# Softmax weights of four key tiles summed on VectorE ahead of one product with ones, in five of sixteen attention steps

## The chip, the cores and the metric

One core of a Trainium2 chip runs the whole kernel in one launch. The time is the device time in microseconds (us) of that core, from launch to end. The kernel before takes 1580.93 us in the median of three runs (1577.99 to 1581.23). Nothing else runs beside it.

The engines of a core work from queues of their own, each in order: TensorE (PE in the profile, with the loads of its stationary operand shown apart as PEld), VectorE (DVE), ScalarE (ACT), GpSimd (POOL) and SyncE (SP), which only issues transfers here.

## What is computed

Two sequences of 1024 rows of 1024 numbers go through half a feed-forward block, an attention block and another half feed-forward block, each behind a layer norm and added to its input:

```python
x = x + 0.5 * ffn(layernorm(x), gate_w, base_w, base_b, lora_A, lora_B)
x = x + attn(layernorm(x), Wq, Wk, Wv, Wo)
x = x + 0.5 * ffn(layernorm(x), gate_w, base_w, base_b, lora_A, lora_B)
```

The feed-forward block is a 1024 x 1024 product with a bias and a low-rank part chosen by a gate. Attention has 32 heads of 32 numbers, 8 key and value heads (four query heads share one), rotary positions and a causal mask:

```python
att = einsum(q, k) / sqrt(32)                # causal, -inf above the diagonal
probs = softmax(att, axis=-1)
out = einsum(probs, v).reshape(B, T, 1024) @ Wo
```

The change lies in the divisor of that softmax: the sum of the exponentials over all keys of a row.

## The kernel before, in words

**Tiles and steps.** The 2 x 1024 rows are 16 tiles of 128 rows, numbered `t` from 0 to 15; tiles 0 to 7 are the first sequence, 8 to 15 the second. The program goes through 17 steps. A step does the attention of one tile, and beside it the dense work of other tiles: the feed-forward of tiles ahead (`stage_a1`), their projections to q, k and v (`stage_a2`), the output projection of the tile before (`stage_c1`) and the last feed-forward of an older tile (`stage_c2`). The strings `NORMAL` and `SEQS` set which pieces go into which step, and `step` hands them out between the units of attention. Tile 8 has its attention last, in step 16.

**A unit of attention** is a tile `t` and one key head `g` with its four query heads. Query tile `t` sees `L = t % 8 + 1` key tiles, so `L` is 4 for tiles 3 and 11, 5 for 4 and 12, and 8 for tile 7. Each unit passes twice over its key tiles:

- `unit_s1` (L634) makes the scores with queries on the partitions (PE, L649; four matmuls for a key tile) and takes their row maxima on VectorE (L666). The maxima are turned and go by four small transfers on SP (L685) into two extra rows of the query operand.
- `unit_s2` (L774) makes the scores the other way round, keys on the partitions, less the maxima (PE, L782), and their exponentials on ScalarE (L788) as a tile `p32` of 128 keys x (4 heads x 128 queries) in 32-bit floats. On the diagonal GpSimd zeroes what is masked (L790).

**Values and divisors.** `av_add` (L747) collects the `p32` tiles of a unit in batches of up to four (`BATCH`). When at least two more key tiles have followed (`SKEW`), `av_batch` (L709) issues the products of a batch as one unbroken run on PE (L727), each held behind the one before. A batch of four key tiles has four products with the values, `(0, VA[..], p32)`, and then products with a matrix of ones, `(1, ones, sums)`, which add up the exponentials over the 128 keys. For the latter, `add_pairs` (L694) first adds the exponentials two key tiles at a time on VectorE (L706) into a buffer `pair`, of which there are two. Such a product is four matmuls, one for a head, each with a stationary operand of 128 x 32 at a column position of its own; in the trace each matmul is two records, so one product is eight records. A key tile left over, without a partner, goes to its ones product as it is. After a unit's last batch, ScalarE copies both results (L734), VectorE takes the reciprocal (L736) and the product (L741), and L742 and L743 split it in halves for the output projection.

**What sets the order.** The order of the instructions on each engine is not that of the text alone. The program is laid out by a scheduler that goes by times it assumes for each instruction, held in places by explicit orders (the run of `av_batch`, and dense work kept behind the L782 matmuls by `behind`). So an instruction more on one engine can move others, also in steps that the edit doesn't name.

**Weights.** The projections' weights lie in device memory in halves of 1 MB and are fetched on SP by `prefetch` (L414, issue L418) into three buffers `ws` in turn. A fetch waits on SP until the products that read its buffer are through. SP carries all other loads too: the query rows (L685), the inputs `xt` (L136) and the stores of results (L819, L821).

Of the kernel before, what the change touches and what calls it, by code (L numbers as in the profile page):

```python
# [13 lines left out]
ALU = mybir.AluOpType  # L14
# [18 lines left out]
AHEAD = 5  # L33
NEARLY = 3
LOFF = 2
NTURN, NTURN2 = 3, 3
TLAG = 12
SB, LB = 3, 2
# [3 lines left out]
def kernel(  # L42
# [16 lines left out]
    nc = tc.nc  # L59
# [574 lines left out]
    def unit_s1(t, g):  # L634
# [8 lines left out]
        for j in reversed(range(L)):  # L643
            ps = p_s1.tile([P, GRP, P], FP, name="s1")
            diag = j == L - 1
            off = diag and L > LOFF
            pem = diag and not off
# [44 lines left out]
    pairs = {}  # L692

    def add_pairs(batch):  # L694

        t, g, L, us = batch
        key = (t, g, us[0][0])
        if key in pairs:
            return
        pairs[key] = []  # L700
        for i in range(0, len(us), 2):
            if i + 1 == len(us):
                pairs[key].append(us[i][1])
                continue
            sums = pp.tile([P, GRP, P], FP, name="pair", bufs=2)
            nc.vector.tensor_tensor(sums, us[i][1], us[i + 1][1], ALU.add)  # L706
            pairs[key].append(sums)

    def av_batch():  # L709

        add_pairs(pend[0])
        t, g, L, us = pend.popleft()
        if us[0][0] == 0:
# [33 lines left out]
    def av_add(t, g, j, L, p32):  # L747

        if not pend or len(pend[-1][3]) == BATCH or pend[-1][0:2] != (t, g):
            pend.append((t, g, L, []))  # L750
        pend[-1][3].append((j, p32))
        after = 0
        while len(pend) > 1:
            after = sum(len(b[3]) for b in list(pend)[1:])
            add_pairs(pend[0])
            if after < SKEW:
                break
            av_batch()
# [367 lines left out]
```

## Time and profile before

| what | value |
|---|---|
| median of three runs | 1580.93 us |
| the profiled execution, its own time | 1578.13 us |
| its span, from first to last instruction | 1576.3 us |
| mean granted TensorE clock | 0.983 |
| busy: PE, DVE, ACT, POOL | 1488.0, 1120.9, 893.6, 381.0 us |
| DMA, mean rate over the span | 136 GB/s |

The profile is taken of one execution. Busy time is a union: two records that overlap on an engine are counted once. The matmuls' ends are modelled and overlap the next ones, so the mean duration of one is longer than its share of the engine; the distance from start to start says what one costs. The chain that ended last is followed back from the last instruction: what it gives as a line's share is the time in which that line's instructions were what the end waited for. A row "A <- B" in the view of the waits says that engine A stood idle until instruction B ended.

The attention steps can be told in the trace by the exponentials at L788, of which tile `t` has 8 x `L`. Step 3 runs from 286.2 to 381.8 us, step 4 to 479.3, step 7 from 696.6 to 871.5, step 11 from 1019.2 to 1116.6 and step 12 to 1214.1.

### The profile page before, as it was taken

Reading aid. Unit: us, or ns where it says so; the run is one execution under the profiler, and the core shown is the slowest. Engines: PE = TensorE matmul, PEld = TensorE weight load, DVE = VectorE, ACT = ScalarE, POOL = GpSimd, SP = SyncE. Lnnn points to the kernel's source line nnn. Section 1 sums busy time; section 2 is a strip of 40 time slices with the busy share of each in tenths; the row PEclk is TensorE's granted clock in tenths of the full one; section 3 lists DMA queues with packets and bytes.
Section 4 is the critical chain, followed back from the end, with each engine's and each line's share of the span. In section 5 each row is a group of like instructions: output and inputs, shape, how many; then the busy total and the mean of one; then the engine's idle time right before and its main releaser. Section 6 shows DMA issues by size and latency. Waiting matters only on the chain.

```text
span 1576.3 us, 38332 instructions
## 1 busy us (share of the span) xinstructions
PE 1488.0 (94%) x15908; PEld 865.4 (55%) x15908; DVE 1120.9 (71%) x2454; ACT 893.6 (57%) x1523; POOL 381.0 (24%) x636
## 2 busy tenths in 40 slices
PE   5898999999999999989999898999999999999998
PEld 3345556555565555656554454655555556566644
DVE  6777668757587686787744575766869688689653
ACT  8575546556466465565642545554746556566731
POOL 3342333222132231221211122222222122221120
PEclk9998999999999999999999999999999999999999
DMA  8943163262522603513526324345170431601241
GB/s 292 327 134 135 55 227 109 70 249 57 216 95 91 232 14 122 189 42 138 188 76 251 121 95 161 122 156 167 44 277 17 181 129 31 248 27 69 82 161 41
DMA packets 57501, 214.25 MB, mean 136 GB/s; under 512 B 19952, under 2 KB 23024, under 8 KB 37872
## 3 DMA queue, kind: packets, MB, share of 16 engines
q1 hardware_dynamic: 51248, 184.54, 32.6%
q0 software_dynamic: 4640, 16.78, 5.8%
q10 hardware_dynamic: 1440, 10.49, 1.6%
q8 instruction: 125, 2.05, 0.5%
q14 instruction: 48, 0.39, 0.1%
HBM read 191.34 MB, written 20.19 MB: 134 GB/s over the span
## 4 chain that ended last, share of the span: by engine, by line
PE 74%; DVE 11%; ACT 7%; issue 2%; DMA 2%; POOL 1%; SPq 0%; DVEq 0%; ACTq 0%; POOLq 0%
PE pd L406 14%; PE pd L407 14%; PE pd L408 14%; PE av L727 11%; PE s L782 6%; PE s L649 6%; DVE mx L666 3%; PE s L332 3%; ACT p L788 2%; DVE bst L382 1%; DMA ws<-wstr 1%; DVE pair L706 1%; DVE o L736 1%; ACT tt L333 1%; DVE ws L208 1%
## 5 line engine op out<-in xcount | busy, mean ns | idle before, releaser
L788 ACT ACTIVATE p<-s,cs 128x512 f32<-128x512 f32 x576 | 378.0, 690 | 163.5 <-PE s L782 160.8
L666 DVE TENSOR_REDUCE mx<-s 128x4 f32<-128x512 f32 x480 | 313.9, 674 | 80.1 <-PE s L649 70.3
L706 DVE TENSOR_TENSOR pair<-p,p 128x512 f32<-128x512 f32 x256 | 178.9, 701 | 80.9 <-ACT p L788 31.4
L782 PE MATMUL s<-qt,kts 98*128 98x512 f16 x576 | 207.4, 387 | 16.8 <-ACT p L788 9.5
L649 PE MATMUL s<-kts,qt 96*128 96x128 f16 x2304 | 210.3, 223 | 11.2 <-DVE mx L666 8.3
L406 PE MATMUL pd<-ws,tt 128*128 128x512 f16 x544 | 206.4, 380 | 2.5 <-DMA ws<-wstr 1.0
L649 PEld LDWEIGHTS <-qt 96*128 96x128 f16 x2304 | 161.4, 99 | 85.4 <-issue 39.9
L407 PE MATMUL pd<-ws,tt 128*128 128x512 f16 x544 | 206.1, 379 | 0.0
L408 PE MATMUL pd<-ws,tt 128*128 128x512 f16 x544 | 205.3, 379 | 0.0
L406 PE MATMUL pd<-wb,tt 128*128 128x512 f16 x512 | 197.8, 386 | 6.3 <-DVE xt L493 4.9
L407 PE MATMUL pd<-wb,tt 128*128 128x512 f16 x512 | 197.1, 385 | 1.3 <-DVE wb L208 1.3
L408 PEld LDWEIGHTS <-tt 128*128 128x128 f16 x1312 | 128.7, 98 | 125.9 <-issue 7.8
L407 PEld LDWEIGHTS <-tt 128*128 128x128 f16 x1312 | 129.5, 99 | 122.3 <-issue 14.3
L408 PE MATMUL pd<-wb,tt 128*128 128x512 f16 x512 | 196.4, 384 | 0.0
L406 PEld LDWEIGHTS <-tt 128*128 128x128 f16 x1312 | 129.0, 99 | 122.1 <-issue 11.3
L727 PE MATMUL av<-p,va 128*32 128x128 f32 x4608 | 167.2, 278 | 5.1 <-POOL p L790 3.8
L727 PEld LDWEIGHTS av<-p,va 128*32 128x32 f32 x4608 | 115.2, 110 | 74.4 <-issue 50.7
L743 POOL TENSOR_TENSOR tt<-o,tt 128x128 f16<-128x128 f32 x128 | 61.3, 479 | 372.3 <-ACT tt L742 366.0
L790 POOL TENSOR_SCALAR_AFFINE_SELECT p<-p 128x512 f32<-128x512 f32 x128 | 82.6, 647 | 260.4 <-ACT p L788 256.4
L736 DVE RECIPROCAL o<-o 128x128 f32<-128x128 f32 x128 | 120.5, 942 | 22.9 <-ACT o L734 22.7
L661 POOL TENSOR_SCALAR_AFFINE_SELECT sm<-sm 128x512 f32<-128x512 f32 x96 | 71.1, 741 | 229.0 <-ACT sm L660 218.6
L333 ACT COPY tt<-s 128x1024 f16<-128x1024 f16 x84 | 84.3, 1019 | 34.3 <-PE s L332 33.8
(203 smaller groups left out, 2175.0 us busy)
## 6 DMA issues: line engine op xcount, KB each, us to landing
ws<-wstr SPq DMA_DIRECT2D x142, 1024.0 KB
xt<-hb POOLq DMA_DIRECT2D x32, 512.0 KB, 5.5
wstr<-ws ACTq DMA_DIRECT2D x9, 1024.0 KB
xt<-in_x_dram SPq DMA_DIRECT2D x16, 512.0 KB
out_dram<-xt SPq DMA_DIRECT2D x15, 512.0 KB
qt<-mt SPq DMA_DIRECT2D x256, 1.0 KB
ws<-in_wb_dram SPq DMA_DIRECT2D x2, 1024.0 KB
qst<-in_wb_dram SPq DMA_DIRECT2D x2, 1024.0 KB
```

The lines of the kernel that those rows point to most:

```text
L333: nc.scalar.copy(out, ps[0:rows])
L406: nc.tensor.matmul(ps, lhsT=th, rhs=wh, start=(k == 0), stop=False)
L407: nc.tensor.matmul(ps, lhsT=th, rhs=wl, start=False, stop=False)
L408: nc.tensor.matmul(ps, lhsT=tl, rhs=wh, start=False, stop=(last and k == KB - 1))
L649: nc.tensor.matmul(ps[:, h, :], lhsT=q[0 : 3 * DH, h, :], rhs=KT[b0 + j][0 : 3 * DH, g, :], start=(not pem or h == 0), stop=not pem,)
L666: nc.vector.tensor_reduce(mx[:, odd, j, :], ps, AX.X, ALU.max)
L706: nc.vector.tensor_tensor(sums, us[i][1], us[i + 1][1], ALU.add)
L727: prev = nc.tensor.matmul(av[rows, i, :], lhsT=w, rhs=p32[:, h, :], start=(us[0][0] == 0 and n == 0), stop=(last and n == len(runs) - 1), ...
L736: nc.vector.reciprocal(rc, rc)
L782: ins = nc.tensor.matmul(ps.rearrange("p h k -> p (h k)"), lhsT=KT[b0 + j][0 : MR + MC, g, :], rhs=q[0 : MR + MC].rearrange("p h k -> p (h ...
L788: nc.scalar.activation(p32, ps, AF.Exp, scale=cs)
L790: nc.gpsimd.affine_select(out=p32, in_=p32, compare_op=ALU.is_ge, fill=0.0, base=0, pattern=[[0, GRP], [1, P]], channel_multiplier=-1,)
```

## The change

In the steps of tiles 3, 4, 7, 11 and 12, when a batch has a second pair, its sum is added to the sum of the first pair, in place, and only the sum of all four key tiles is kept for a product with ones.

```diff
+QUAD = [3, 4, 7, 11, 12]
...
             sums = pp.tile([P, GRP, P], FP, name="pair", bufs=2)
             nc.vector.tensor_tensor(sums, us[i][1], us[i + 1][1], ALU.add)
+            if i == 2 and t in QUAD:
+                nc.vector.tensor_tensor(sums, sums, pairs[key].pop(), ALU.add)
             pairs[key].append(sums)
```

Line numbers in the text are those of the kernel before. In the changed kernel the lines below the new constant are one further down, the new addition is its L709, and what follows it is three further down (the matmuls of `av_batch` at L730).

## Prediction

> **What bounds the kernel now.** I read the busy shares first, then the chain that ended last, then the steps of the change, then the lines that it touches.
>
> ```profile
> PE 1488.0 (94%) x15908; PEld 865.4 (55%) x15908; DVE 1120.9 (71%) x2454; ACT 893.6 (57%) x1523; POOL 381.0 (24%) x636
> ...
> PE 74%; DVE 11%; ACT 7%; issue 2%; DMA 2%; POOL 1%; SPq 0%; DVEq 0%; ACTq 0%; POOLq 0%
> PE pd L406 14%; PE pd L407 14%; PE pd L408 14%; PE av L727 11%; PE s L782 6%; PE s L649 6%; DVE mx L666 3%; PE s L332 3%; ACT p L788 2%; DVE bst L382 1%; DMA ws<-wstr 1%; DVE pair L706 1%; DVE o L736 1%; ACT tt L333 1%; DVE ws L208 1%
> ```
>
> TensorE holds the end: it is busy for 94% and carries 74% of the chain. L727, the line that loses work, is on the chain for 11%; L706, which is like the line that gains work, for 1%. An average over stages doesn't say this of the five steps, so next the busy times by stretch (steps 3, 4, 7, 11 and 12; columns: sum of the stretch, PE, PEld, DVE, ACT, POOL, clock, DMA share and rate):
>
> ```profile
> 286.20:381.80 95.60, 92.21 (x998) 54.23 (x997) 68.33 (x157) 49.95 (x92) 24.59 (x42) 1.00 0.41 139
> 381.80:479.30 97.50, 96.02 (x1096) 56.44 (x1095) 73.33 (x164) 58.67 (x101) 23.03 (x38) 1.00 0.39 131
> ...
> 696.60:871.50 174.90, 168.30 (x1731) 96.05 (x1729) 111.24 (x248) 87.75 (x144) 29.60 (x50) 0.99 0.46 150
> ...
> 1019.20:1116.60 97.40, 92.83 (x1008) 54.76 (x1006) 69.02 (x161) 53.88 (x97) 26.59 (x45) 1.00 0.39 131
> 1116.60:1214.10 97.50, 96.01 (x1096) 56.42 (x1095) 73.26 (x164) 58.61 (x100) 23.06 (x38) 1.00 0.40 131
> ```
>
> In steps 4 and 12 TensorE stands idle for 1.5 us of 97.5; in the others for 3.4, 6.6 and 4.6. VectorE has 24 to 64 us free in each (64 to 75% busy). So TensorE is short of time in just these steps and VectorE is not, on the mean.
>
> **What goes from TensorE.** All five tiles have `L` of 4, 5 or 8, so their batches of four are 1, 1, 2, 1 and 1 for each of eight units: 8 + 8 + 16 + 8 + 8 = 48. Each loses one product with ones, four matmuls or eight records: 384 of the 2048 records on `pair`.
>
> ```profile
> L706 DVE TENSOR_TENSOR pair<-p,p 128x512 f32<-128x512 f32 x256 | 178.9, 701 | 80.9 <-ACT p L788 31.4 <-POOL p L790 23.0 <-PE av L727 21.6
> ...
> L727 PE MATMUL av<-pair,ones 128*32 128x128 f32 x2048 | 87.2, 276 | 3.4 <-DVE pair L706 3.3
> ```
>
> The busy row would give 87.2 / 256 = 0.34 us for a product, but contains each run's tail. A run in the timeline shows what one costs in the flow: 32 records (four products) start at 309.43 and the next line's at 310.32.
>
> ```profile
> 309.43 1.08 PE L727 MATMUL av<-p,va 128*32 128x128 f32 x32
> ...
> 310.32 0.62 PE L727 MATMUL av<-pair,ones 128*32 128x128 f32 x16
> ...
> 310.88 0.39 PE L406 MATMUL pd<-ws,tt 128*128 128x512 f16 x1
> ```
>
> That is 0.89 / 4 = 0.22 us a product. The Trainium skill ("TensorE: Matmul & The Clock Gate", Measured speedup vs the span model) prices column-packed matmuls at the duration of one and some 4 ns for each further one: with the row's 276 ns, about 0.29 us, an estimate for a group that stands alone. By it the 48 products are 13.8 us, by the timeline 48 x 0.22 = 10.6. Groups follow each other here without a gap, so I take 10.6.
>
> How much of it reaches the end? L727 has 576 products with values, 256 with pair sums and 64 with single tiles: 896 x 0.22 = 197 us of flow. Its 11.4% of the chain (the chain in order of time gives the decimal) is 180 us: 0.91. So the gain is 10.6 x 0.91 = **-9.6 us**. The earlier end of a run also brings L734 forward; that is in this figure.
>
> **What comes onto VectorE.** 48 additions of 128 x 512 floats, the form of L706: 48 x 0.70 = 33.6 us busy; back to back they start 0.60 us apart, 28.8 us. Steps 4 and 12 go from 75 to 81%. In the order of the changed program's instructions 11 of the 48 stand straight behind the second pair addition, 14 behind one further instruction, the rest behind two to seven, mostly maxima of L666. What does it cost? Three ways to say it:
>
> - By share: DVE is 11% of the chain, 173 us of its 1121 busy: 0.155. 33.6 x 0.155 = 5.2 us.
> - By L706's own share: 0.9%, or 14.2 of 178.9 us: 0.08, which gives 2.7 us.
> - By slack: from the trace I took, for each of the 48 batches, the time from the end of its second pair addition to the start of the ones product. In 41 it is over 0.8 us and swallows 0.60. In 5 it is 0.05 us (TensorE was waiting) and in 2 it is 0.66. So if nothing moves, TensorE waits 5 x 0.60 = 3.0 us more. Behind it in TensorE's queue stand the unbroken run's end and the dense matmuls of L406 to L408.
>
> Then what is queued behind an addition on VectorE: the maxima of L666, for which L649 waits 8.3 us in all today, the normalisation's steps, and the turned maxima whose transfers (L685) L782 awaits (5.4 us). I put 1.2 us on that and take **+4.2 us** in all, between 2.7 and 5.2. Not below zero, as nothing is taken from VectorE; above, up to rival A.
>
> Against the change speaks the Trainium skill ("GPSIMD Engine Reference", Specifications): VectorE's instructions with two SBUF inputs contend with GpSimd for its interface to SBUF, and such is each new addition. The rows: `pair` took 683 ns in the median, 1136 at most. POOL is busy for 17 to 27% in the five steps. If a quarter of 48 took the longest time, VectorE would lose 12 x 0.45 = 5.4 us, at 0.155 some 0.8 on the path; L706's mean of 701 against 683 makes it 0.9 us in all, 0.1 on the path. The mean is already in my sum, so I add nothing.
>
> **What moves.** Two `pair` buffers serve all batches, and L706 stood idle for 21.6 us until L727 freed one, 8.7 of it in step 7:
>
> ```profile
> DVE pair L706 <- PE av L727: 8.7, 6, 2.1
> ```
>
> With the sum in place the first buffer is free after 0.7 us on VectorE instead of after TensorE's run. Half of the 8.7 would go, at 0.155: **-0.6 us**.
>
> The scheduler also lays out other instructions anew. On SP, which loses none and gains none, one input load (L136) goes behind one weight fetch (L418) around step 5, a fetch and one group of L685 change places before step 9, and from tile 11 on some fetches stand before or behind a group of L685. A fetch waits for its buffer (12.0 us at the longest), and what stands behind it waits along: for L685 this is L782, for L136 the norm of a tile ahead. TensorE waits for these now for 1.0 us (L406) and 5.4 us (L782), so each direction is good for a few us. Moves on PE, ACT, POOL reach into steps 5, 6 and 13 to 15; steps 9 and 10 keep their order. With no row that gives them a sign I cost them at 0, from -4 to +4.
>
> **Sum.** -9.6 + 4.2 - 0.6 + 0 = **-6.0 us**. The profiled execution took 1578.13 us (span 1576.3), so 1572.1 for its like. It lies 2.8 below the median of the runs, so against 1580.93 I predict **1574.9 us**. About 0.2%, 3.2 us, can be told from no change.
>
> **Rivals.**
>
> A. *VectorE's additions make TensorE wait (slower).* The order on TensorE is fixed: a late quad sum holds the ones product, and all dense matmuls behind it. Each short batch costs 0.60 us. The gain of 10.2 is used up at 17 short batches of 48 and turned to over 3.2 lost at 23; five are short now. For: VectorE goes over 80% in steps 4 and 12, its queue is in order, and on 37 of the 48 the quad sum stands behind further work. Against: 41 have over 0.8 us of slack and TensorE is the later one. With 27 short: 16.2 - 10.2 = +6, 1587 us. Chance 0.21, moves that go against the change counted in.
>
> B. *The time is lost again at another wait (no change).* In steps 3 and 11 TensorE has idle spots that the removed matmuls don't touch: in step 11 it waits 0.81 us for a weight fetch, and the chain there follows transfers for about 5%. If steps 3 and 11 give nothing, 16 of the 48 products are lost, 3.2 us of the 9.6: -2.8, so 1578 us. A clock drop at a new pause belongs here: the clock was granted by half for 3.4 or 6.8 us at some step ends, which costs 1.7 or 3.4 us a time. Chance 0.19.
>
> C. *VectorE takes it all in its idle time.* Then -10.6 to -11, 1570 us. For: steps 4 and 12, where TensorE pauses for 1.5%. Against: the five short batches. Chance 0.15.
>
> That the change does nothing is ruled out by the program's order: 192 matmuls fewer on TensorE, 48 additions more on VectorE.
>
> **How the numbers follow.** My forecast has 0.45, from -8.5 to -3.5 us; it and C are faster: 0.60. B is the same, 0.19; A is slower, 0.21. The range reaches from C with moves in favour, 1566, to A at 1587 with half of A's chance beyond about 1586: 1566 to 1586. The likeliest sign's own range is 1567 to 1577.
>
> **What would show it.** The records on `pair` and ones fall to 1664 and their busy time by 10 to 16 us; the new addition has 48 rows of about 0.70 us. PE's busy time falls by some 10 us while its idle time stays: right. The waits of L727 for VectorE (3.3 us at the product, 5.4 at its weight load) should rise by about 3 us; by over 10 would be A. Steps 4 and 12 should each be shorter by 1 to 1.6 us and step 7 by 2 to 3. If the steps 5, 6 and 13 to 15, where only the order moved, change by more than these, my cost of 0 for the moves was wrong; so it would be if the waits for `ws` and `qt` grew by several us.

## The result, and the profile after

The changed kernel takes 1586.71 us in the median of five runs (1584.62 to 1589.10), the kernel before 1579.84 us beside it: a ratio of 1.0048, 95% interval 1.0032 to 1.0063. It is slower by some 7 us where 6 us of gain were forecast, and outside the range of 1566 to 1586. The profiled execution took 1589.1 us (span 1587.4), 2.4 us above that median.

The page of the changed kernel (its lines are one further down above the edit and three below it): busy times, then the chain that ended last.

```profile
PE 1481.6 (93%) x15524; PEld 853.8 (54%) x15524; DVE 1152.5 (73%) x2502; ACT 893.1 (56%) x1523; POOL 386.7 (24%) x636
...
PE 71%; DVE 15%; ACT 6%; issue 2%; DMA 2%; POOL 1%; SPq 1%; DVEq 0%; ACTq 0%; POOLq 0%
PE pd L407 13%; PE pd L408 13%; PE pd L409 13%; PE av L730 10%; PE s L785 6%; PE s L650 6%; DVE mx L667 4%; PE s L333 3%; ACT p L791 2%; DVE pair L707 1%; DVE bst L383 1%; DMA ws<-wstr 1%; DVE o L739 1%; DVE ws L209 1%; DVE xt L494 1%
```

TensorE lost 384 records, as it should, and 6.4 us of busy time in all; VectorE has 48 instructions and 31.6 us more, and its share of the chain has gone from 11 to 15%. The groups of the touched lines agree with the sum of the prediction: products of pair sums from 87.2 to 76.9 us, 48 additions of 728 ns.

```profile
L730 PE MATMUL av<-pair,ones 128*32 128x128 f32 x1664 | 76.9, 278 | 2.2 <-DVE pair L707 1.7 <-DVE pair L709 0.2
...
L709 DVE TENSOR_TENSOR pair<-pair 128x512 f32<-128x512 f32 x48 | 35.0, 728 | 0.4
```

So the work is what was forecast, and it is not the products that wait for the new sums: their line waits 2.2 us in all, 3.4 before. The busy times by stretch (steps 3, 4, 7, 11, 12, 14 and 16 of the changed kernel) say where the time went.

```profile
286.40:385.40 99.00, 94.76 (x957) 54.18 (x956) 76.76 (x174) 51.01 (x93) 28.48 (x42) 1.00 0.40 134
385.40:478.00 92.60, 89.83 (x996) 52.19 (x995) 71.70 (x156) 56.37 (x97) 22.16 (x36) 1.00 0.40 138
698.50:871.80 173.30, 166.90 (x1603) 91.92 (x1601) 119.72 (x264) 87.66 (x144) 33.03 (x50) 0.99 0.46 151
1017.80:1124.10 106.30, 96.10 (x959) 54.84 (x957) 76.91 (x176) 54.76 (x97) 27.58 (x45) 0.98 0.36 120
1124.10:1217.40 93.30, 90.41 (x1006) 53.16 (x1004) 73.42 (x160) 56.54 (x98) 22.48 (x36) 1.00 0.40 137
1321.10:1421.40 100.30, 96.03 (x1185) 57.35 (x1183) 77.18 (x144) 58.77 (x101) 20.30 (x32) 0.93 0.39 119
1506.60:1587.40 80.80, 71.58 (x524) 34.65 (x522) 33.96 (x86) 21.24 (x43) 12.77 (x24) 0.98 0.30 98
```

The same view of the kernel before, for the last two of them, which the change doesn't name:

```profile
1318.00:1414.80 96.80, 93.09 (x1178) 56.75 (x1177) 74.02 (x140) 58.09 (x101) 18.72 (x32) 0.95 0.39 124
1499.50:1576.30 76.80, 69.97 (x525) 34.28 (x522) 34.03 (x86) 21.32 (x43) 12.88 (x24) 1.00 0.32 103
```

Steps 3 and 4 together went from 193.1 to 191.6 us and step 7 from 174.9 to 173.3; steps 11 and 12 together from 194.9 to 199.6. Steps 14 and 16, in which no work has changed, lost 3.5 and 4.0. In step 11 TensorE is now idle for 10.2 us of 106.3, 4.6 of 97.4 before. The waits of TensorE that grew, before and after:

```profile
PE s L782 <- ACT p L788: 9.5, 35, 0.6
...
PE s L649 <- DVE mx L666: 8.3, 20, 1.4
```

```profile
PE s L650 <- DVE mx L667: 14.6, 24, 2.0
...
PE s L785 <- ACT p L791: 13.0, 43, 1.4
...
PE pd L407 <- DMA ws<-wstr: 6.4, 2, 3.7
```

The scores wait longer for VectorE's maxima to free their buffers, and TensorE waits 6.4 us for two weight fetches (1.0 before, in the row of L406), 3.7 of it in step 11 and 2.7 in step 16. The one in step 16, before and after:

```profile
1536.31 0.38 PE L406 MATMUL pd<-ws,tt 128*128 128x512 f16 x1 [0.23 <-DMA ws<-wstr]
...
1545.77 0.56 PE L407 MATMUL pd<-ws,tt 128*128 128x512 f16 x1 [2.67 <-DMA ws<-wstr]
1546.12 0.63 PE L408 MATMUL pd<-ws,tt 128*128 128x512 f16 x1
1546.55 0.63 PE L409 MATMUL pd<-ws,tt 128*128 128x512 f16 x1
```

SP issues this fetch 31.2 us into step 16 in both kernels; it lands 2.4 us later in the changed one. Behind the pause the granted clock stands at half for 3.41 us, and the matmuls start 0.43 us apart, 0.22 at the full clock. Together that is step 16's loss of 4.0 us: TensorE is idle for 2.4 us more and, with the same work, busy for 1.6 us more. In step 14 the clock is at half for 13.1 us instead of 9.9, which is worth some 1.6 of the 3.5 us.

Two things lie on top of each other: the work has changed, and the order of nearly everything with it. The experiments take them apart.

### The profile page after: what moved, and what is told of

Its sections match the earlier page's. It is cut to its first block, busy times and chain, and to the rows that moved or that the text cites. A ratio compares the mean times of both kernels' runs of the same rounds, so it can differ in the third digit from the quotient of the medians.

```text
span 1587.4 us, 37598 instructions
## 1 busy us (share of the span) xinstructions
PE 1481.6 (93%) x15524; PEld 853.8 (54%) x15524; DVE 1152.5 (73%) x2502; ACT 893.1 (56%) x1523; POOL 386.7 (24%) x636
## 4 chain that ended last, share of the span: by engine, by line
PE 71%; DVE 15%; ACT 6%; issue 2%; DMA 2%; POOL 1%; SPq 1%; DVEq 0%; ACTq 0%; POOLq 0%
PE pd L407 13%; PE pd L408 13%; PE pd L409 13%; PE av L730 10%; PE s L785 6%; PE s L650 6%; DVE mx L667 4%; PE s L333 3%; ACT p L791 2%; DVE pair L707 1%; DVE bst L383 1%; DMA ws<-wstr 1%; DVE o L739 1%; DVE ws L209 1%; DVE xt L494 1%
## 5 line engine op out<-in xcount | busy, mean ns | idle before, releaser
L730 PE MATMUL av<-p,va 128*32 128x128 f32 x4608 | 167.4, 279 | 2.2 <-POOL p L793 2.2
L793 POOL TENSOR_SCALAR_AFFINE_SELECT p<-p 128x512 f32<-128x512 f32 x128 | 87.1, 682 | 305.2 <-ACT p L791 301.4
L730 PEld LDWEIGHTS av<-p,va 128*32 128x32 f32 x4608 | 116.3, 110 | 64.2 <-issue 45.0
L746 POOL TENSOR_TENSOR tt<-o,tt 128x128 f16<-128x128 f32 x128 | 65.0, 508 | 296.2 <-ACT tt L745 289.6
```

The costliest lines, as they stand in the source:

```text
L730: prev = nc.tensor.matmul(av[rows, i, :], lhsT=w, rhs=p32[:, h, :], start=(us[0][0] == 0 and n == 0), stop=(last and n == len(runs) - 1), ...
L793: nc.gpsimd.affine_select(out=p32, in_=p32, compare_op=ALU.is_ge, fill=0.0, base=0, pattern=[[0, GRP], [1, P]], channel_multiplier=-1,)
```

## The experiments

Theory O: the new layout of the order costs what is lost, the exchange of products for additions gains. Theory D, rival A of the prediction: the additions make TensorE wait, in any order. To tell them apart, several kernels hold every engine to a given order. Behind the traced program each instruction gets an edge, without a wait, to the one ahead of it in a table taken from the program before or after:

```diff
+    for e, q in queues.items():
+        prev = None
+        for k in q:
+            for i in [mine[e][k]] + behind_it.get((e, k), []):
+                if prev is not None:
+                    tc.add_manual_dep(i, prev.name, NOSYNC, reason="order")
+                prev = i
```

The code is shortened: `NOSYNC` stands for the kind of the edge. Every ratio below is to runs of the kernel before on the same chip, five rounds each; its median was 1580.66, 1580.23 and 1580.49 us in the three groups (runs 1 to 4, 5 to 8, 9 to 12). Differences in us are the ratio less 1, times that median; the difference of the two medians lies up to 2 us from it, in run 2 up to 3. Lengths of single steps come from one profiled execution of each kernel.

**1. The change in the old order.** The edit of the change, with the table of before.

> The change in full, but every other instruction is held on its engine in the order that it has in the kernel before; each of the 48 new additions stands straight behind its second pair addition. Theory O (the loss comes from the new layout of the order, the exchange of products for additions itself gains): about 6 us faster than before, 1574 us. Theory D (the additions on VectorE make TensorE wait, whatever the order): 5 to 10 us slower, 1585 to 1590 us.

Measured: 1592.15 us, ratio 1.006 (1.0041 to 1.0079). Theory O falls: the exchange itself loses 9.5 us. In the profile steps 3, 4, 7, 11 and 12 are longer by 3.2, 1.6, 0.4, 1.8 and 1.7 us, all others together by 0.4 us.

**2. The old work in the new order.**

```diff
-            if i == 2 and t in QUAD:
-                nc.vector.tensor_tensor(sums, sums, pairs[key].pop(), ALU.add)
```

> The work of the kernel before, all pair sums and all products with ones, with no new addition, but on each engine in the order of the changed kernel; the 48 products that the change removes stand at the end of their runs. Theory O: 10 to 14 us slower than before, 1590 to 1594 us. Theory D: within 3 us of before.

Measured: 1609.46 us, ratio 1.0164 (1.0139 to 1.0189), worse than either theory said. The new order is made for the smaller runs of products, and the old work in it is not a fair price of the order as a whole. But the steps whose work is the same in all of these kernels can be compared. Steps 14 and 16 of this run:

```profile
1342.10:1442.40 100.30, 96.02 (x1183) 57.37 (x1182) 77.49 (x145) 58.73 (x100) 20.34 (x32) 0.93 0.38 119
1527.60:1608.30 80.70, 71.62 (x524) 34.61 (x522) 34.02 (x86) 21.30 (x43) 12.86 (x24) 0.98 0.30 98
```

They are as long as in the changed kernel (100.3 and 80.8), although no addition was made anywhere; with the old order they take 95.9 and 76.9 us in run 1. So these 7 to 8 us go with the layout. In step 16 TensorE waits 2.5 us for the same fetch as in the changed kernel, and the half clock follows.

**3. Additions alone, in the old order.** Products kept; in place of the addition:

```diff
-                nc.vector.tensor_tensor(sums, sums, pairs[key].pop(), ALU.add)
+                nc.vector.tensor_tensor(sums, sums, sums, ALU.max)
```

> The order of before with 48 more VectorE instructions of the new additions' size and place (each takes the larger of a pair sum and itself, which changes nothing), and no product removed: the price of the additions alone. Theory O: 3 to 5 us slower, as in my sum. Theory D: 15 to 20 us slower.

Measured: 1593.05 us, ratio 1.0072 (1.0055 to 1.009): 11.4 us, where the prediction had 4.2. TensorE's waits:

```profile
PE s L650 <- DVE mx L667: 11.3, 22, 1.4
...
PEld av L730 <- DVE pair L709: 6.9, 10, 1.1
...
PE av L730 <- DVE pair L709: 4.8, 8, 0.9
```

**4. Fewer products alone, in the old order.**

```diff
+            if i == 2 and t in QUAD:
+                pairs[key].pop()
```

(Not shown: in the 48 batches the second pair addition takes a form that adds the 1 as well. Its mean time is 700 ns, the plain one's 701.)

> The order of before with the 48 products removed and no new addition: the divisor leaves out the first pair of key tiles of these batches, and 1 is added to each weight of the second pair so that it can't be zero. The gain of TensorE alone. Both theories: 9 to 11 us faster, 1569 to 1571 us. Much less would mean that TensorE's time in these steps was not what the end waits for.

Measured: 1578.90 us, ratio 0.9981 (0.9965 to 0.9996), 3.0 us, where 9 to 11 were expected. The runs lie far apart (1572.24 to 1583.73); the profiled one, the fastest, has the five steps shorter by 5.1 us in all. By either number at most half of the 10.6 us of TensorE's flow comes back.

Runs 3 and 4 together make +8.4 us, run 1 measured +9.5 (6.5 to 12.5 by its interval): the exchange adds up. Theory D was now read as "VectorE is as scarce in these steps as TensorE: about a third of each addition's 0.7 us is on the path" (theory V), and tried from both sides.

**5. Additions on GpSimd.**

```diff
-                nc.vector.tensor_tensor(sums, sums, pairs[key].pop(), ALU.add)
+                nc.gpsimd.tensor_tensor(sums, sums, pairs[key].pop(), ALU.add)
```

> The change in full in the order of before, but the 48 additions on GpSimd, each at the place in its queue that the trace of before gives to the end of the second pair addition. Theory V (VectorE's time is as scarce in these steps as TensorE's, some 0.24 us of each addition lies on the path): the 11 us of the additions go, unless GpSimd's longer time for an addition (1.4 us or more, from its 0.65 us for a mask of this size and 0.79 us for 256 elements) makes the products wait or slows VectorE: 1577 to 1584 us. If the price lies in the products' wait for a later sum, not in VectorE's queue, it is at least that of the additions on VectorE: 1590 us or more.

Measured: 1598.05 us, ratio 1.0112 (1.0093 to 1.0131). VectorE is freed of them, and it is worse. The groups show why:

```profile
L732 PE MATMUL av<-pair,ones 128*32 128x128 f32 x1664 | 76.4, 277 | 15.4 <-POOL pair L709 12.3 <-DVE pair L707 2.9
...
L709 POOL TENSOR_TENSOR pair<-pair 128x512 f32<-128x512 f32 x48 | 62.1, 1294 | 59.0 <-DVE pair L707 38.3 <-DVE m L674 6.9 <-DVE nv L450 5.9
```

An addition takes 1294 ns there, and the products wait for it. Against theory V this decides nothing: one cost has taken the other's place.

**6. Additions only where VectorE stood idle.** From the trace of before: in 27 of the 48 batches VectorE is idle for 0.6 us or more between the end of the second pair addition and the start of the product. Only these add four key tiles, at the idle spot, in the old order.

```diff
-            if i == 2 and t in QUAD:
+            if i == 2 and key in USE:
```

> The order of before; four key tiles are added only in those 27 of the 48 batches in which VectorE stood idle for 0.6 us or more between the second pair addition and the product, and the addition is put at that idle spot. Theory V: the additions cost little there and 27 of 48 products' gain stays: 1577 to 1580 us. If an addition costs the same wherever it stands (11 us for 48, so 6 for 27, less some 2 for the products): 1584 to 1586 us.

Measured: 1574.81 us, ratio 0.9971 (0.9959 to 0.9984): faster than both kernels, with the full form and time of the additions:

```profile
L709 DVE TENSOR_TENSOR pair<-pair 128x512 f32<-128x512 f32 x27 | 19.5, 723 | 0.6
```

**7. VectorE relieved.** First pair addition of the 48 batches cut to a tiny instruction, all products kept.

```diff
+            if t in QUAD and len(us) == BATCH and i == 0:
+                nc.vector.tensor_tensor(us[0][1][:, :, 0:2], us[0][1][:, :, 0:2], us[0][1][:, :, 0:2], ALU.max)
+                pairs[key].append(us[0][1])
+                continue
```

> The reverse: in the order of before, with every product with ones kept, the first pair addition of the 48 batches is cut to a tiny one of 128 x 8 and the product takes the first key tile alone (the divisor leaves out the second key tile of these batches, and 1 is added to each weight of the second pair). VectorE is relieved of 48 x 0.5 us, TensorE does the same as before. Theory V: 5 to 10 us faster, 1571 to 1576 us. If TensorE alone sets the pace of these steps: within 2 us of before.

Measured: 1584.60 us, ratio 1.002 (1.0007 to 1.0032). Taking 25 us from VectorE gains nothing, which speaks against theory V. The run is not clean, though: the tiny instruction writes the first key tile in place, so that products with values now wait for it (1.1 us at the product, 1.6 at its weight load). In its profile steps 4 and 11 are longer by 1.8 and 2.6 us, with 0.9 and 1.6 us of waiting for weight fetches.

**8. New order as far as step 10, old order behind it**, with the change in full.

> The change in full, on each engine in the new order as far as step 10 and in the order of before behind it. By the profiles' lengths of the steps the new order costs 3 us in steps 5 and 6 and some 8 us in steps 14 and 16 where no work is changed, and gives back some 5 us in 3 and 4. If that holds, 1580 to 1584 us, 3 to 6 us less than the change in its own order; if the order matters little, 1586 to 1590 us.

Measured: 1584.13 us, ratio 1.0024 (1.0012 to 1.0035): 3.8 us slower than before against 7.6 for the change, so about half of the loss goes with the new order of the last steps. Step 16 is back at 76.6 us, step 14 at 97.9.

What was left is theory P: an addition costs by its place, nothing in an idle spot, its full time and more in front of what TensorE is about to need. Runs 9 and 10 set it against a uniform price.

**9. The other 21 batches**, straight behind the second pair addition, the 27 left as before.

> The complement of the run with the idle spots: in the order of before, only the other 21 of the 48 batches (in which VectorE had no idle spot of 0.6 us ahead of the product) add four key tiles, straight behind the second pair addition. Theory P (an addition costs by its place: nothing in an idle spot, its full time and more in front of work that TensorE is about to need): all of the loss of the 48 in the old order lies here, 10 to 14 us slower, 1590 to 1594 us. Theory V (a share of VectorE's time, the same for each): 21/48 of it, 4 to 5 us slower, 1585 us.

Measured: 1593.72 us, ratio 1.0075 (1.0057 to 1.0094). The 21 carry the whole loss, 11.9 us. TensorE waits longer for maxima (8.3 us before), and for the new sums:

```profile
PE s L650 <- DVE mx L667: 12.6, 27, 1.4
...
PE av L732 <- DVE pair L709: 4.2, 7, 0.9
```

One of them, the first batch of step 3, in the timeline of before and then of this run:

```profile
293.13 0.68 DVE L706 TENSOR_TENSOR pair<-p,p 128x512 f32<-128x512 f32 x1
...
293.73 0.20 DVE L384 BATCH_NORM_AGGREGATE mv<-bst 128x2 f32<-128x12 f32 x1
...
293.87 0.64 PE L727 MATMUL av<-pair,ones 128*32 128x128 f32 x16
293.87 0.68 DVE L666 TENSOR_REDUCE mx<-sm 128x4 f32<-128x512 f32 x1
```

```profile
293.33 0.68 DVE L707 TENSOR_TENSOR pair<-p,p 128x512 f32<-128x512 f32 x1
...
294.05 0.69 DVE L709 TENSOR_TENSOR pair<-pair 128x512 f32<-128x512 f32 x1
...
294.66 0.20 DVE L385 BATCH_NORM_AGGREGATE mv<-bst 128x2 f32<-128x12 f32 x1
...
294.79 0.43 PE L732 MATMUL av<-pair,ones 128*32 128x128 f32 x8 [0.20 <-DVE pair L709]
294.81 0.68 DVE L667 TENSOR_REDUCE mx<-sm 128x4 f32<-128x512 f32 x1
```

Counted from the start of the second pair addition, the product starts after 0.74 us before and after 1.46 in this run, and with it the dense matmuls behind; a norm's statistics and a maximum, which others await, have gone back from 0.60 and 0.74 us to 1.33 and 1.48. One product of 0.22 us was saved. This batch is one of the five that the prediction counted as short. The other 16 of the 21 have 0.85 to 5.05 us between the sum and the product in the trace of before, but no idle spot of 0.6 us within it: VectorE has other work there, and an addition puts that work back.

**10. The 27 additions in idle spots, no product removed.**

> The order of before with 27 instructions of an addition's size (each takes the larger of a pair sum and itself, which changes nothing) in the 27 idle spots, and no product removed. Theory P: within 2 us of before. Theory V: 27/48 of the 11 us that all 48 cost, 6 to 7 us slower.

Measured: 1581.58 us, ratio 1.0005 (0.9994 to 1.0016). No cost can be told from nothing (-0.9 to +2.5 us), where a price per addition gave 6 to 7. With run 9 this rules a uniform price out and fits theory P. Batch and spot differ together between the two runs. Run 1 less run 9 puts the 27, straight behind their pair additions, at -2.4 us, so most of it seems to lie in the choice of the batch; no run tests the spot alone.

**11. Idle spots of all steps:** 47 batches of 96.

> As the 27 in idle spots, but over all steps: 47 of the 96 batches with two pairs have an idle spot of 0.6 us, and add four key tiles there, in the order of before. Theory P: the gain of 5 us of the 27 grows with the count to 7 to 9 us, 1571 to 1573 us. Theory V: 1580 us or more.

Measured: 1576.23 us, ratio 0.9966 (0.9952 to 0.998). Faster, but not clearly better than the 27 (-5.4 us against -4.6): the growth to 7 to 9 us that was expected did not come.

**12. The 27, with the scheduler's own order.**

> The same 27 batches add four key tiles, but the scheduler lays out the order by its own times, nothing is held. If the new layout is a part of the loss by itself, it takes back the 5 us or more: 1580 to 1586 us. If the choice of the batches is enough: 1574 to 1577 us.

Measured: 1575.57 us, ratio 0.9967 (0.9956 to 0.9979). The choice of the batches is enough; a new layout isn't bad as such. In its profile steps 5 and 16 are again long (108.4 and 80.1 us, 105.5 and 76.7 before; in 16 the same fetch is late, by 2.1 us), and steps 3, 10 and 11 shorter.

**What the clock adds.** Every execution has its mean granted clock on record. What is missing from 1, times the execution's time, is the most that half-clock stretches can have cost it. An estimate from these, as means over all executions against those of the kernel before in the same group:

| run | difference, us | of it the clock at most, us |
|---|---|---|
| 1, change in the old order | +9.5 | +3.7 |
| 2, old work in the new order | +25.9 | +6.6 |
| 3, additions alone | +11.4 | +2.7 |
| 4, fewer products alone | -3.0 | +3.6 |
| 5, additions on GpSimd | +17.7 | +10.0 |
| 6, 27 in idle spots | -4.6 | -1.2 |
| 7, VectorE relieved | +3.2 | +1.8 |
| 8, new order to step 10 | +3.8 | +0.6 |
| 9, other 21 | +11.9 | +5.5 |
| 10, 27 additions alone | +0.8 | -0.7 |
| 11, 47 in idle spots | -5.4 | +2.4 |
| 12, 27 in their own order | -5.2 | +0.4 |

So up to a quarter (run 3) to about a half (runs 5 and 9) of a loss is TensorE at half clock, and without it the gains of runs 4 and 11 would be up to 6.6 and 7.8 us. Runs 9 and 10 stay apart (+6.4 and +1.5). Why the clock is lower in these runs is seen only in single places, such as the pause in step 16 above.

## Why the prediction was wrong

- *TensorE loses 48 products of 0.22 us:* right. 384 records fewer, 10.3 us less busy on them.
- *0.91 of that reaches the end, -9.6 us:* wrong. Run 4 gives -3.0 us (-5.5 to -0.6), and up to 3.6 us of what is missing is the lower clock, which the prediction had under rival B and not in its sum. The share of L727 in one chain says what that chain would save if nothing else came up; with the products gone, other waits follow within the same step. In run 4's profile the idle time of TensorE in steps 4 and 12 rises from 1.5 to 2.3 us. That the 21 batches without an idle spot gain nothing, because there VectorE is late anyhow, fits (the 27 gain 4.6 us in run 6, all 48 no more in run 4), but is only argued.
- *Additions cost +4.2 us:* the step that failed most. Run 3: 11.4. It was priced by means, 0.155 or 0.08 of VectorE's time, or by the products' lag, five short batches of 0.60. The lag was the right view with the wrong question: it counted as slack any time between sum and product, also where VectorE had other work queued in it. So it had five batches short, where 21 have no idle spot. Asked for idle time of 0.6 us, the same trace gives 27 batches whose additions cost 0.05% and 21 whose exchange costs 0.75% (runs 10 and 9). Its 0.60 us was also the distance of unrelated additions; the new one starts 0.72 us behind the sum that it reads.
- *The moves at 0, -4 to +4:* on the whole this held, step by step it did not. By the prediction's own signs it failed: steps 5 and 14 are longer by 2.3 and 3.5 us, and the waits for `ws` went from 1.0 to 6.4 us. Run 2 shows some 8 us lost to the layout in steps 14 and 16; between the changed kernel and run 1 it gives back about 7 us in the five steps (+1.6 against +8.6 us by the profiles). By the ratios the two layouts can't be told apart for this work (1.0048 and 1.006, with intervals that overlap); run 8, a mixture, has the lowest (1.0024).
- *The freed pair buffer, -0.6 us:* the idle time of L706 for it fell from 21.6 to 12.6 us; no run prices this alone.
- *GpSimd's contention, nothing added:* the new additions took 728 ns against 701 for their model, 1.3 us in all. Right to leave out; whether contention makes these 27 ns, no run here shows.
- *Rival A* named the side and, at 1587 us, the size, which is in part luck. Its place was right in the old order (run 3: 6.9 and 4.8 us of waits for the new sums) but not in the changed kernel, where the waits of L727 for VectorE, product and weight load together, fell from 8.7 to 6.5 us instead of rising by 3; there the maxima and two weight fetches are late.

What stays open: why relieving VectorE made the kernel slower (run 7), why the fetch of step 16 lands later in the new layouts, why the clock is lower in run 4, and the profiles against the medians: one profiled execution lies up to 7 us from its kernel's median (run 4: 1572.24 against 1578.90), so lengths of steps say where, and only the ratios how much.

## What to carry to other kernels

In this kernel work moved from a full engine to one that is idle for a quarter of the time was free only where the idle time lay between the moved work's input and its reader: count such idle spots in the trace of before, instance by instance, and leave the rest as they are. An engine's share of the chain, or its busy share, prices neither the gain nor the loss of such an exchange: here the gain was a third of what they gave and the loss nearly three times it. Where a scheduler lays out the order, price the edit in a held order and the new order apart. And look at the granted clock of every execution: pauses of TensorE can come back a second time as half clock.

## What was not expected

- A 128 x 512 addition in 32-bit floats took 1294 ns on GpSimd (run 5) and 728 on VectorE (the changed kernel), with the same operands.
- 27 additions of 0.72 us, 19.5 us of work, can be put into a program with no change to its time that can be told (1.0005), while 21 of the same form in other places, each with a product saved, cost 11.9 us.
- With the order held, undisturbed steps come out alike to 0.1 us: step 1 took 78.4 or 78.5 us, step 2 48.3 and step 15 84.7 in before and in runs 1, 3, 6, 9 and 10. Others don't: step 6, with no changed work, took 111.8 in before and 112.1 to 113.5 in these. The clock stands at half for 2.6 us of it in before and for 6.3 to 7.7 us in these.
